# Other statistics, other chore slots and another split of the residual parts in a two-layer attention kernel

## The chip, the cores and the metric

The kernel runs on one core of a Trainium2 chip, in one launch. The metric is the time on the device in microseconds. A run of the kernel before takes 3205.84 us, the median of three runs (3205.17 to 3208.25). A core has five engines with a queue of instructions each: TensorE (PE; its weight loads are PEld), VectorE (DVE), ScalarE (ACT), GpSimd (POOL) and SyncE (SP). They wait for one another through semaphores, and the DMA transfers that SP and POOL issue run beside them.

## The reference

Two layers of the same kind are applied to x, 8 images of 512 channels by 32 x 32 pixels (1024 positions). All is float32. Cut to what matters, one layer is:

```python
xg = x.reshape(B, 8, -1)
xn = ((xg - xg.mean(-1)) * rsqrt(xg.var(-1) + 1e-5)).reshape(B, C, H, W) * gamma + beta
q, k, v = products of xn (512 channels) with wq, wk, wv (512 x 512), plus biases
attn = softmax(q.k / sqrt(64))          # 8 heads of 64 channels, 1024 x 1024 each
x = x + proj_w @ (attn @ v) + proj_b    # residual
```

The output is x after the second layer.

## The kernel before

**Jobs.** `jobs` lists 16 pairs of image and layer: images in twos, for each two both images in layer 0 and then both in layer 1. For every job n the main loop runs an attention and then the products of the next job: `v_phase` for V, and `deep_phases` for the output projection O of job n and for K and Q of job n + 1. The attention of job n is 64 iterations (8 groups of a pair of heads and half of the positions, 8 key blocks each): TensorE multiplies scores, ScalarE takes the exponential (L875, tile e), VectorE adds the exponentials up (L885, L887, tile acc), TensorE multiplies with the values (L901). At the end of a group VectorE reduces acc (L917) and adds the halves of the result (L924, into q). For each second group the row sums are brought together by small DMAs (r<-r, L944), VectorE inverts them (first L948), and they go out and back through rd and rb.

**Chores.** `put(i, fn)` hangs other work on iteration i of the attention, or on the next free one. This is how the next job's normalization is spread: `reads` (statistics of x and their gather), then `steps` (groups, factors, four applies that write xn), then the sums that the fast products need. Statistics come from VectorE (`stat`, BNStats on 512 positions, eight for each job), or for job 1 from ScalarE (`sums` and `squares`, four each, L244 and L252). `gather` sends them through DRAM: two DMAs mv to dm and one from dm to gm (L279), which waits for both. `groups` (L286 and after) works on gm and sends the result back as mr. In attentions 0 to 2 there are also factors for later use: `first_factors` loads blocks of a weight, VectorE makes four sums and differences of them (128 x 512, L154 to L160), and `store_factors` writes them to DRAM.

**Products.** O, K and Q are computed by a Strassen-like scheme at two levels: seven outer products, each a chain of seven inner ones. A set of 21 chains runs on TensorE, with two chains interleaved; chain c writes its result to tile p_c (128 x 1024) of the pool `epool`, tag e, which has six buffers and is shared with the exponentials. In a chain ScalarE writes three quarters of p (L646, L648) and copies one inner product to s, and VectorE writes the other quarters (L653, or L655 with a bias). When a chain's weights are used for the first time, `prepare` makes their inner differences on VectorE (four of 128 x 128, L154 to L160) and stores them as `deep`. Weights come from a ring of seven buffers.

**Residual.** The seven O tiles p_0 to p_6 (outer products 1, 2, 6, 5, 7, 3 and 4) are summed into quarters (oh, sh) of x. `end(c)` lists for each chain what it adds: `add` is a VectorE sum of two tiles (L668), `more(oh, sh, part)` adds part to a quarter of x, by VectorE (L684), or with `moved=True` by a DMA issued from GpSimd that accumulates in x (L682). VectorE's sums are put in the queue `outer`, and a thunk takes one of it after the inner products 7 and 3 of a chain, that is two for each chain. If `soon` (sums for O's right-hand sides) has something, that goes first; if `outer` is empty, `extra` is next: statistics of job n + 2 from chain 15 on, and after the attention of job 1 the loads and sums (L1081) of the second layer's output bias.

**Order.** Each engine runs its instructions in the order in which the program makes them. A tile of a pool can be written again only when its readers, DMAs too, are done; that is where waits on a buffer come from.

Of the kernel before, what the change touches and what calls it, by code (L numbers as in the profile page):

```python
# [28 lines left out]
NT = S // P  # L29
HALF = S // 2  # L30
HP = NH // 2
NVEC = 6 * NC
GAMMA, BETA, BQ, BK, BP, BV = (i * NC for i in range(6))
SUM_LIMIT = 1e10
# [38 lines left out]
def fast_path(  # L73
# [85 lines left out]
        else:  # L159
            nc.vector.tensor_sub(w[:, S4], w[:, A12], w[:, S2])  # L160

    def store_factors(w, layer, which):
        keep = wdram.tile([P, NW, 2, CH], F32, name=f"keep_{which}_{layer}")
        if (which, layer) == (O, 1):
            nc.sync.dma_start(keep, w)
        else:
            for s in (slice(S1, NW), slice(S3, S3 + 1)):
                nc.sync.dma_start(keep[:, s], w[:, s])
        factors[which, layer] = keep

    plan, held, raw = deque(), {}, set()
# [183 lines left out]
    def norm_steps(n):  # L355
        norm = Norm(n)

        def place():
            xn[0] = acts.tile([P, NC, S], F32, tag="xn", name=f"xn_{n}")

        def factors():
            norm.factors(slice(0, NC))
            if n > 1:
                place()

        if n == 1:
            reads = [place] + [lambda cc=cc: norm.sums(cc) for cc in range(NC)]
            reads.append(norm.less_mean)
            reads += [lambda cc=cc: norm.squares(cc) for cc in range(NC)]
            reads.append(lambda: (norm.by_count(), norm.gather()))  # L370
            return reads, [norm.groups, factors] + [lambda cc=cc: norm.apply(cc) for cc in range(NC)]
        reads = [lambda cc=cc, sh=sh: norm.stat(cc, sh) for cc in range(NC) for sh in range(2)]
        reads.append(norm.gather)
        steps = [norm.groups, factors] + [lambda cc=cc: norm.apply(cc) for cc in range(NC)]
        return reads, steps
# [198 lines left out]
    def deep_phases(n, extra, outs=None, early=()):  # L574
# [11 lines left out]
        def begin(c):  # L586
# [6 lines left out]
                (kt if which == K else qt)[0] = dst[which]  # L593
            if c + 2 < len(chains):
                ahead, oo = chains[c + 2]
                prepare((job(ahead), ahead, oo))
            if which == O and c in (3, 4):
                soon.extend(outs.steps(c + 2))
            e = epool.tile([P, 2, HALF], F32, tag="e", name=f"p_{n}_{c}")
# [59 lines left out]
        def end(c):  # L659
# [10 lines left out]
            if which == O:  # L670
                b, layer = jobs[m]
                xt = xs[b]

                def more(oh, sh, part, moved=False):


                    cols = slice(sh * HALF, (sh + 1) * HALF)
                    to_ = xt[:, 2 * oh : 2 * oh + 2, cols]

                    def go():  # L680
                        if moved:
                            nc.gpsimd.dma_start(to_, p(part), accum_op=ALU.add)  # L682
                        else:
                            nc.vector.tensor_add(to_, to_, p(part))  # L684
                        parts[oh, sh] -= 1
                        if layer == 1 and parts[oh, sh] == 0:
                            rows = slice(oh * CH, (oh + 1) * CH)
                            later(8.0 if moved else 2.0, lambda: nc.sync.dma_start(
                                out[b, rows, cols].rearrange("(c p) s -> p c s", p=P), to_
                            ))  # L690

                    if moved:
                        go()
                    else:
                        outer.append(go)

                if o == 1:
                    more(0, 0, 1, True)
                elif o == 2:
                    more(0, 0, 2, True)  # L700
                elif o == 6:
                    add(p(6), p(6), p(1))
                    more(0, 1, 6)
                elif o == 5:
                    more(0, 1, 5)
                    more(1, 1, 5, m in (0, 2))
                elif o == 7:
                    add(p(7), p(7), p(6))
                    more(1, 0, 7)
                    more(1, 1, 7)  # L710
                elif o == 3:
                    more(0, 1, 3, True)
                elif o == 4:
                    more(1, 0, 4, True)
                return
# [17 lines left out]
                add(quarter(1, 0), p(7), p(4))  # L733

        live, parts = {}, {(0, 0): 2, (0, 1): 3, (1, 1): 2, (1, 0): 2}
        soon, outer = deque(early), deque()

        def thunk(c, j):
            def go():
                if j == 0:  # L740
                    live[c] = begin(c)
                order = LAST_ORDER if c + 1 == len(chains) else ORDER
                live[c](order[j])
                if order[j] in (7, 3):
                    if soon:
                        soon.popleft()()
                    elif outer:
                        outer.popleft()()
                    elif extra and extra[0][0] <= c:
                        extra.popleft()[1]()  # L750
                if j == 6:
                    end(c)
                    if c + 1 == len(chains):
                        while outer:
                            outer.popleft()()
                advance(0.43)

            return go
# [334 lines left out]

        return load, [lambda oc=oc: add_up(oc) for oc in range(NC)]

    def first_factors(put, which_layers):

        box = []

# [3 lines left out]
                load_blocks(box[0][:, i], layer, which)  # L1103

        put(2, start)
        at = 9
        for i, (which, layer) in enumerate(which_layers):
            for part in range(4):
                at += 3
                put(at, lambda i=i, part=part: factor(box[0][:, i], part))  # L1110
            put(at + 1, lambda i=i, which=which, layer=layer: store_factors(
                box[0][:, i], layer, which
            ))

    deep_x, deep_t = [None], [None]
# [160 lines left out]
    for n in range(-1, len(jobs)):  # L1276
        last = n + 1 == len(jobs)
        outs = None
        if n >= 0:
# [10 lines left out]
                    put(44 + 3 * i, fn)  # L1290
            else:
                if n == 0:
                    first_factors(put, [(O, 0), (V, 1)])
                elif n == 1:
                    first_factors(put, [(K, 1), (Q, 1)])
                elif n == 2:
# [1 line left out]
                for i, (_, fn) in enumerate(extra):  # L1298
                    put(2 + i, fn)
                at = (10, 19, 22, 24, 26, 28, 36, 39, 42, 45)  # L1300
                if n == 0:
                    for i, fn in zip((3, 3, 4, 5, 6, 8, 10, 11, 12, 13, 15), reads):
                        put(i, fn)
                    at = (22, 30, 34, 35, 37, 38, 41, 44, 47, 50)
                for i, fn in zip(at, steps + sums(n + 1)):
                    put(i, fn)
                deep_first = deep_steps(n + 1)
                for at, fn in zip((52, 54, 57, 59), deep_first[4:]):
                    put(at, fn)
                put(61, lambda: (extend_plan(n + 1), [fetch() for _ in range(RING)]))  # L1310
            assert max(chores, default=0) < NT * len(att.groups)
# [16 lines left out]
            extra = deque()  # L1328
            if jobs[n][1] == 1 and jobs[n][0] + 2 < B:
                extra.append((11, lambda b=jobs[n][0] + 2: (x_tile(b), load_x(b))))  # L1330
            if n == 1:
                load, bias_steps = make_out_bias(1)
                extra.append((8, load))
                extra.extend((11, fn) for fn in bias_steps)
            if n + 2 < len(jobs):
                reads, steps = norm_steps(n + 2)
                extra.extend((15, fn) for fn in reads)
        both = deep_phases(n + 1, extra, outs, deep_first[:4] if outs else ())
        both[0]()
        rest[0]()  # L1340
# [259 lines left out]
```

## Time and profile before

Times in us, from the profiled execution. A stage reaches from the first exponentials of one attention to those of the next.

| What | Value |
|---|---|
| Profiled execution, its own time | 3206.06 |
| Its span | 3204.3 |
| Start, to the first attention | 81.57 |
| Attention of job 4 and the products after it (887.72 to 1085.57) | 197.85, TensorE busy all of it |
| Last stage (3064.17 on) | 140.83, TensorE busy 134.40 |
| Exponential L875, 128 x 1024 | 1024 of them, 1025 ns each |
| Sum of exponentials L887, 128 x 1024 | 768 of them, 1219 ns each |
| Sum of two product tiles L668, 128 x 1024 | 94 of them, 1214 ns each |
| Accumulating DMA x<-p, 512 KB | 62 of them, 6.9 from issue to landing in the median |

A row of the windows used below gives the length of a stretch and the busy time of each engine in it. A stage longer than its TensorE work holds waits of TensorE. Busy times of other engines count only where TensorE waits for them.

### The profile page before, as it was taken

The numbers are of one execution on the slowest core, as the hardware profiler recorded it, in microseconds if no ns is written. First come the engines' busy times: TensorE is split into PE (matmuls) and PEld (weight loads), VectorE is DVE, ScalarE is ACT, GpSimd is POOL, SyncE is SP. The second block draws the span as 40 slices with busy tenths as digits, with TensorE's granted clock in tenths as the row PEclk, the third lists the DMA queues.
The fourth block names the chain that finished last, engine by engine and source line by source line (L and its number), as shares of the span: only waits on it lengthen the run. The fifth ranks groups of instructions, "written<-read, shape, count | busy, mean of one in ns | idle before, by whom it ended". The sixth has DMA issues, their size and how long they took to land.

```text
span 3204.3 us, 57789 instructions
## 1 busy us (share of the span) xinstructions
PE 3185.3 (99%) x22917; PEld 1862.8 (58%) x22917; DVE 2772.8 (87%) x3989; ACT 1914.4 (60%) x3063; POOL 100.7 (3%) x95
## 2 busy tenths in 40 slices
PE   9999999999999999999999999999999999999999
PEld 7366384563836638366483754837547375573744
DVE  8897999979889798897988879888898888978878
ACT  4746646466565665656656565565656656566564
POOL 0000000000000000000000000000000000000000
PEclk9999999999999999999999999999999999999999
DMA  8234172350613305034170421504316051150611
GB/s 291 74 107 127 48 213 70 92 169 22 210 28 88 91 26 159 22 100 132 33 211 16 114 72 33 152 16 135 103 44 194 16 137 48 49 136 16 174 37 42
DMA packets 156998, 308.32 MB, mean 96 GB/s; under 512 B 34104, under 2 KB 60592, under 8 KB 156464
## 3 DMA queue, kind: packets, MB, share of 16 engines
q1 hardware_dynamic: 139856, 272.05, 26.8%
q0 software_dynamic: 16864, 32.51, 6.2%
q8 instruction: 181, 2.97, 0.4%
q14 instruction: 97, 0.79, 0.1%
HBM read 225.13 MB, written 45.68 MB: 85 GB/s over the span
## 4 chain that ended last, share of the span: by engine, by line
PE 95%; DVE 3%; DMA 1%; issue 0%; POOL 0%; ACT 0%; DVEq 0%; ACTq 0%; POOLq 0%
PE sc L870 28%; PE po L901 27%; PE zd L636 10%; PE vd L636 10%; PE z L494 6%; PE yd L636 5%; PE ud L636 4%; PE v L494 2%; PE y L494 2%; PE u L494 1%; PE z_last L814 0%; DMA x<-p 0%; DVE w L156 0%; DMA w<-deep 0%; DVE p L655 0%; DVE v L520 0%
## 5 line engine op out<-in xcount | busy, mean ns | idle before, releaser
L875 ACT ACTIVATE e<-sc 128x1024 f32<-128x1024 f32 x1024 | 1045.3, 1025 | 563.4 <-PE sc L870 457.4
L870 PE MATMUL sc<-q,k 64*64 64x512 f32 x8192 | 1058.0, 589 | 0.0
L901 PE MATMUL po<-e,v 64*64 64x512 f32 x8192 | 1057.1, 589 | 0.0
L887 DVE TENSOR_TENSOR acc<-acc,e 128x1024 f32<-128x1024 f32 x768 | 936.0, 1219 | 58.8 <-ACT e L875 12.1
L901 PEld LDWEIGHTS po<-e,v 64*64 64x64 f32 x8192 | 312.9, 133 | 566.0 <-issue 554.4
L870 PEld LDWEIGHTS sc<-q,k 64*64 64x64 f32 x8192 | 311.2, 133 | 562.7 <-issue 545.0
L885 DVE TENSOR_TENSOR acc<-e,e 128x1024 f32<-128x1024 f32 x128 | 156.3, 1221 | 112.3 <-ACT e L875 112.2
L636 PE MATMUL zd<-deep,w 128*128 128x256 f32 x860 | 241.1, 380 | 3.8 <-DVE p L653 1.7
L636 PE MATMUL vd<-deep,w 128*128 128x256 f32 x804 | 224.3, 380 | 2.1 <-DVE p L655 1.3
L636 PEld LDWEIGHTS zd<-deep,w 128*128 128x128 f32 x860 | 162.8, 190 | 28.2 <-DVE p L653 3.0
L636 PEld LDWEIGHTS vd<-deep,w 128*128 128x128 f32 x804 | 152.3, 190 | 24.6 <-DVE p L655 2.5
L917 DVE TRANSPOSE_TENSOR_REDUCE r<-acc 128x32 f32<-128x1024 f32 x128 | 158.5, 1238 | 0.6
L682 POOL DMA_DIRECT2D x<-p x62 | 74.6, 1211 | 1972.7 <-ACT p L646 1525.2
L636 PE MATMUL vd<-os,w 128*128 128x256 f32 x420 | 118.1, 380 | 1.6 <-DVE p L655 1.5
L668 DVE TENSOR_TENSOR p<-p,p 128x1024 f32<-128x1024 f32 x94 | 114.2, 1214 | 0.0
L494 PE MATMUL z<-w,t 128*128 128x256 f32 x480 | 110.9, 379 | 0.0
L494 PE MATMUL z<-w,xn 128*128 128x256 f32 x480 | 110.1, 382 | 0.0
L518 ACT COPY v<-z 128x512 f32<-128x512 f32 x32 | 18.8, 586 | 148.7 <-PE z L494 148.7
L494 PEld LDWEIGHTS z<-w,xn 128*128 128x128 f32 x480 | 90.0, 190 | 23.8 <-issue 12.2
L442 ACT COPY ud<-zd 128x256 f32<-128x256 f32 x156 | 55.7, 357 | 76.6 <-PE zd L636 75.1
L653 DVE TENSOR_TENSOR p<-vd,s 128x256 f32<-128x256 f32 x63 | 26.7, 424 | 85.6 <-PE vd L636 85.6
L657 ACT COPY s<-vd 128x256 f32<-128x256 f32 x156 | 58.1, 373 | 69.2 <-PE vd L636 69.2
(242 smaller groups left out, 4194.9 us busy)
## 6 DMA issues: line engine op xcount, KB each, us to landing
w<-deep SPq DMA_DIRECT2D x287, 448.0 KB, 3.8
x<-p POOLq DMA_DIRECT2D x62, 512.0 KB, 6.9
rb<-rd SPq DMA_DIRECT2D x96, 256.0 KB, 4.0
w<-keep SPq DMA_DIRECT2D x84, 256.0 KB, 2.7
deep<-w SPq DMA_DIRECT2D x42, 448.0 KB, 3.8
w<-wqkv_dram SPq DMA_DIRECT2D x57, 256.0 KB, 2.8
x<-x_dram SPq DMA_DIRECT2D x28, 512.0 KB, 6.4
out_dram<-x SPq DMA_DIRECT2D x28, 512.0 KB, 6.2
```

Source lines behind the costliest of these rows:

```text
L442: nc.scalar.copy(u, z)
L494: nc.tensor.matmul(ps[:, ti * CH : (ti + 1) * CH], right(src, tx[0], o)[:, cc, t0 : t0 + P], w[:, cc, :], start=(start and ti == 0 and cc ...
L636: nc.tensor.matmul(ps, lhs[:, FACTOR[i], :], moving[i], start=start, stop=True, skip_group_check=True,)
L657: return chain(product, lambda ps: nc.scalar.copy(s5, ps), put, z, y, u, w)
L668: outer.append(lambda: nc.vector.tensor_add(to_, a, b))
L682: nc.gpsimd.dma_start(to_, p(part), accum_op=ALU.add)
L870: nc.tensor.matmul(sc[h * HD : (h + 1) * HD, j, :], k[r, hp, k0 : k0 + HD], q[r, hp, sh * HALF : (sh + 1) * HALF], start=True, stop=True,)
L875: nc.scalar.activation(e, sc, AF.Exp, scale=SCALE)
L885: nc.vector.tensor_add(acc[g], self.es[i - 1], e)
L887: nc.vector.tensor_add(acc[g], acc[g], e)
L901: nc.tensor.matmul(po[g][j * HD : (j + 1) * HD, h, :], v[r, kc, d0 : d0 + HD], e[r, j, :], start=(kc == 0), stop=(kc == NT - 1),)
L917: nc.vector.tensor_reduce(self.r[:, 0, m, :], self.acc.pop(g).rearrange("p j (b e) -> p (j b) e", e=RP), AX.X, ALU.add, apply_transpose=True,)
```

## The change

It has these parts:

- Job 3's statistics too come from ScalarE (`ALONE`), and the chore positions that go with that are used for both jobs, 1 and 3. Several of them are a little earlier, and in attention 0 the sums for the next products come at 39 to 45 and 47 to 53.
- In attention 0 the factors are made at every second chore from 8 on, no longer every third from 12; `store_factors` issues these stores, and those of the later attentions, on GpSimd's queue.
- After the attention of job 0, x's quarter (0, 0) gets its first part by VectorE, (0, 1) gets part 5 by DMA and (1, 1) gets part 5 by VectorE. Parts by DMA are no longer issued at once where another part of the same quarter is still waiting in `outer`; they keep their place behind it (`waiting`, `free`).
- Preparations of K's and Q's weights go to a queue `made`, which is served after inner product 7; `soon` and `outer` are served after 3, or when `made` is empty.
- The second layer's output bias is loaded and summed after the attention of job 0, no longer of job 1.

```diff
@@ -29,6 +29,7 @@
 NT = S // P
 HALF = S // 2
 HP = NH // 2
+ALONE = (1, 3)
 NVEC = 6 * NC
 GAMMA, BETA, BQ, BK, BP, BV = (i * NC for i in range(6))
 SUM_LIMIT = 1e10
@@ -159,13 +160,13 @@
         else:
             nc.vector.tensor_sub(w[:, S4], w[:, A12], w[:, S2])
 
-    def store_factors(w, layer, which):
+    def store_factors(w, layer, which, queue=nc.sync):
         keep = wdram.tile([P, NW, 2, CH], F32, name=f"keep_{which}_{layer}")
         if (which, layer) == (O, 1):
-            nc.sync.dma_start(keep, w)
+            queue.dma_start(keep, w)
         else:
             for s in (slice(S1, NW), slice(S3, S3 + 1)):
-                nc.sync.dma_start(keep[:, s], w[:, s])
+                queue.dma_start(keep[:, s], w[:, s])
         factors[which, layer] = keep
 
     plan, held, raw = deque(), {}, set()
@@ -360,10 +361,10 @@
 
         def factors():
             norm.factors(slice(0, NC))
-            if n > 1:
+            if n not in ALONE:
                 place()
 
-        if n == 1:
+        if n in ALONE:
             reads = [place] + [lambda cc=cc: norm.sums(cc) for cc in range(NC)]
             reads.append(norm.less_mean)
             reads += [lambda cc=cc: norm.squares(cc) for cc in range(NC)]
@@ -593,7 +594,11 @@
                 (kt if which == K else qt)[0] = dst[which]
             if c + 2 < len(chains):
                 ahead, oo = chains[c + 2]
-                prepare((job(ahead), ahead, oo))
+                key = (job(ahead), ahead, oo)
+                if key in raw and n > 0 and ahead != O:
+                    made.append(lambda: prepare(key))
+                else:
+                    prepare(key)
             if which == O and c in (3, 4):
                 soon.extend(outs.steps(c + 2))
             e = epool.tile([P, 2, HALF], F32, tag="e", name=f"p_{n}_{c}")
@@ -683,27 +688,32 @@
                         else:
                             nc.vector.tensor_add(to_, to_, p(part))
                         parts[oh, sh] -= 1
+                        waiting[oh, sh] -= 1
                         if layer == 1 and parts[oh, sh] == 0:
                             rows = slice(oh * CH, (oh + 1) * CH)
                             later(8.0 if moved else 2.0, lambda: nc.sync.dma_start(
                                 out[b, rows, cols].rearrange("(c p) s -> p c s", p=P), to_
                             ))
 
-                    if moved:
+                    waiting[oh, sh] += 1
+                    if not moved:
+                        outer.append(go)
+                    elif waiting[oh, sh] == 1:
                         go()
                     else:
                         outer.append(go)
+                        free.append(go)
 
                 if o == 1:
-                    more(0, 0, 1, True)
+                    more(0, 0, 1, m > 0)
                 elif o == 2:
                     more(0, 0, 2, True)
                 elif o == 6:
                     add(p(6), p(6), p(1))
                     more(0, 1, 6)
                 elif o == 5:
-                    more(0, 1, 5)
-                    more(1, 1, 5, m in (0, 2))
+                    more(0, 1, 5, m == 0)
+                    more(1, 1, 5, m == 2)
                 elif o == 7:
                     add(p(7), p(7), p(6))
                     more(1, 0, 7)
@@ -733,7 +743,8 @@
                 add(quarter(1, 0), p(7), p(4))
 
         live, parts = {}, {(0, 0): 2, (0, 1): 3, (1, 1): 2, (1, 0): 2}
-        soon, outer = deque(early), deque()
+        waiting, free = dict.fromkeys(parts, 0), []
+        soon, outer, made = deque(early), deque(), deque()
 
         def thunk(c, j):
             def go():
@@ -742,10 +753,16 @@
                 order = LAST_ORDER if c + 1 == len(chains) else ORDER
                 live[c](order[j])
                 if order[j] in (7, 3):
-                    if soon:
+                    if made and order[j] == 7:
+                        made.popleft()()
+                    elif soon:
                         soon.popleft()()
                     elif outer:
                         outer.popleft()()
+                        while outer and outer[0] in free:
+                            outer.popleft()()
+                    elif made:
+                        made.popleft()()
                     elif extra and extra[0][0] <= c:
                         extra.popleft()[1]()
                 if j == 6:
@@ -1093,7 +1110,7 @@
 
         return load, [lambda oc=oc: add_up(oc) for oc in range(NC)]
 
-    def first_factors(put, which_layers):
+    def first_factors(put, which_layers, at=9, apart=3):
 
         box = []
 
@@ -1103,13 +1120,12 @@
                 load_blocks(box[0][:, i], layer, which)
 
         put(2, start)
-        at = 9
         for i, (which, layer) in enumerate(which_layers):
             for part in range(4):
-                at += 3
+                at += apart
                 put(at, lambda i=i, part=part: factor(box[0][:, i], part))
             put(at + 1, lambda i=i, which=which, layer=layer: store_factors(
-                box[0][:, i], layer, which
+                box[0][:, i], layer, which, nc.gpsimd
             ))
 
     deep_x, deep_t = [None], [None]
@@ -1290,7 +1306,7 @@
                     put(44 + 3 * i, fn)
             else:
                 if n == 0:
-                    first_factors(put, [(O, 0), (V, 1)])
+                    first_factors(put, [(O, 0), (V, 1)], 6, 2)
                 elif n == 1:
                     first_factors(put, [(K, 1), (Q, 1)])
                 elif n == 2:
@@ -1298,14 +1314,14 @@
                 for i, (_, fn) in enumerate(extra):
                     put(2 + i, fn)
                 at = (10, 19, 22, 24, 26, 28, 36, 39, 42, 45)
-                if n == 0:
+                if n + 1 in ALONE:
                     for i, fn in zip((3, 3, 4, 5, 6, 8, 10, 11, 12, 13, 15), reads):
                         put(i, fn)
-                    at = (22, 30, 34, 35, 37, 38, 41, 44, 47, 50)
+                    at = (22, 30, 34, 35, 36, 37, 39, 41, 43, 45)
                 for i, fn in zip(at, steps + sums(n + 1)):
                     put(i, fn)
                 deep_first = deep_steps(n + 1)
-                for at, fn in zip((52, 54, 57, 59), deep_first[4:]):
+                for at, fn in zip((47, 49, 51, 53) if n == 0 else (52, 54, 57, 59), deep_first[4:]):
                     put(at, fn)
                 put(61, lambda: (extend_plan(n + 1), [fetch() for _ in range(RING)]))
             assert max(chores, default=0) < NT * len(att.groups)
@@ -1328,13 +1344,14 @@
             extra = deque()
             if jobs[n][1] == 1 and jobs[n][0] + 2 < B:
                 extra.append((11, lambda b=jobs[n][0] + 2: (x_tile(b), load_x(b))))
-            if n == 1:
+            if n == 0:
                 load, bias_steps = make_out_bias(1)
-                extra.append((8, load))
-                extra.extend((11, fn) for fn in bias_steps)
+                extra.append((9, load))
+                extra.extend((12, fn) for fn in bias_steps)
             if n + 2 < len(jobs):
                 reads, steps = norm_steps(n + 2)
-                extra.extend((15, fn) for fn in reads)
+                if n + 2 not in ALONE:
+                    extra.extend((15, fn) for fn in reads)
         both = deep_phases(n + 1, extra, outs, deep_first[:4] if outs else ())
         both[0]()
         rest[0]()
```

## The prediction

> **What bounds the kernel now.** I read the page first, its span, its engines and its chain of waits:
>
> ```profile
> span 3204.3 us, 57789 instructions
> PE 3185.3 (99%) x22917; PEld 1862.8 (58%) x22917; DVE 2772.8 (87%) x3989; ACT 1914.4 (60%) x3063; POOL 100.7 (3%) x95
> ...
> PE 95%; DVE 3%; DMA 1%; issue 0%; POOL 0%; ACT 0%; DVEq 0%; ACTq 0%; POOLq 0%
> ...
> x<-p POOLq DMA_DIRECT2D x62, 512.0 KB, 6.9
> ```
>
> TensorE sets the end. So I cut the span at the first exponential of each attention and took busy time by stage (window, length, then PE, PEld, DVE, ACT, POOL, clock, DMA share, GB/s):
>
> ```profile
> 81.57:287.13 205.56, 199.89 (x1435) 115.30 (x1437) 179.02 (x274) 127.34 (x208) 8.25 (x6) 1.00 0.37 107
> 287.13:489.78 202.65, 199.95 (x1435) 115.30 (x1437) 188.52 (x311) 119.63 (x192) 6.22 (x5) 1.00 0.40 122
> 489.78:689.87 200.09, 198.76 (x1435) 115.67 (x1437) 178.16 (x270) 119.72 (x192) 7.43 (x6) 1.00 0.40 124
> 689.87:887.72 197.85, 197.85 (x1434) 115.85 (x1437) 170.54 (x238) 119.73 (x192) 6.22 (x5) 1.00 0.34 99
> ```
>
> Each row is the same TensorE work, one attention and the products after it. From the fourth on it takes 197.85 us with TensorE never idle. The first three exceed this by 7.71, 4.80 and 2.24: 14.75 us together, 0.46% of the run. The change moves work in these three alone (TensorE's order is untouched), so no gain can pass 14.75 us. The waits of TensorE in the first two windows (total, times, longest):
>
> ```profile
> PE zd L636 <- DVE p L653: 1.7, 2, 1.1
> PE v L494 <- DVE q L924: 1.7, 1, 1.7
> PE zd L636 <- ACT yd L438: 1.6, 1, 1.6
> PE vd L636 <- DVE p L655: 0.6, 1, 0.6
> ```
>
> ```profile
> PE vd L636 <- DVE p L655: 1.1, 3, 0.6
> PE zd L636 <- DVE p L655: 0.7, 1, 0.7
> PE zd L636 <- DVE p L653: 0.6, 1, 0.6
> ```
>
> These total less than the excess, since a stalled matmul also looks longer; start-to-start distances of TensorE against the usual 0.216 us give the rest. Then VectorE in attention 0, VectorE in the second set of products, and GpSimd's transfers in both sets:
>
> ```profile
> DVE lt L948 <- DMA r<-r: 2.5, 1, 2.5
> ```
>
> ```profile
> 440.66 1.21 DVE L684 TENSOR_TENSOR x<-x,p 128x1024 f32<-128x1024 f32 x1
> 441.80 0.47 DVE L655 SCALAR_TENSOR_TENSOR p<-ud,out_step,s 128x256 f32<-128x256 f32 x1
> 442.19 1.21 DVE L684 TENSOR_TENSOR x<-x,p 128x1024 f32<-128x1024 f32 x1
> 443.32 0.28 DVE L154 TENSOR_TENSOR w<-w 128x128 f32<-128x128 f32 x1
> ```
>
> ```profile
> 235.10 2.44 POOL L682 DMA_DIRECT2D x<-p  x2 [9.55 <-DVE os L539]
> 240.77 1.20 POOL L682 DMA_DIRECT2D x<-p  x1 [3.23 <-ACT p L648]
> 245.59 1.20 POOL L682 DMA_DIRECT2D x<-p  x1 [3.62 <-ACT p L648]
> ```
>
> ```profile
> 442.81 1.20 POOL L682 DMA_DIRECT2D x<-p  x1 [9.05 <-ACT yd L438]
> 447.93 1.20 POOL L682 DMA_DIRECT2D x<-p  x1 [3.92 <-DVE w L156]
> ```
>
> VectorE lies end to end at 440 us: two big adds (1.13 us each from start to start) and a weight preparation (four differences, 0.93 us with their waits) for every chain of seven products, which takes TensorE 3.02 us.
>
> [...] the second row agrees (199.95 busy where 197.85 is needed), so I count window lengths. [...] The trace has 6.9 in the median and 7.7 to 11.0 in the first set, and I use these. [...]
>
> **The change, part by part.**
>
> *Attention 0.* The stores of factors leave SP's queue, the r gather of L944 is no longer behind the wait for dm's landing, and the 2.5 us wait at L948 goes. Squares, gather() and groups() move: by_count and gather go from chore 16 to 21, groups from 23 to 24. Groups thus comes 3 iterations (1.72 us each, 5.1 us) after gather. In the trace the first dm was issued at 110.43, gm at 116.76 (it waits for dm's landing) and gm takes some 2.3 us to land: 8.6 us, and a set of rd and rb DMAs now stands between the dm issues on SP. I place gm's landing at 130.4 to 131.9, VectorE at L286 at 124.7: a new wait of 5.7 to 7.2 us, queued in front of every acc add. Factors done sooner fill idle time that VectorE had before. The last acc add (195.61 in the trace) then comes at 196.9 to 198.4, as VectorE is never idle after the wait. The V products wait for it: TensorE loses 3.1 to 4.6 us where it lost 1.93; I take 3.8. Late acc adds hold e's buffers for some 0.5 (0.1 to 1.0). Moving the stores itself I cost at nothing: GpSimd is idle there (3%); if not hidden, 1.2 us of GpSimd each, which nobody awaits.
>
> *First products (0 to 1).* Gone: p_6's write waiting for the transfer of p_1 (1.84 on TensorE with its restart) and quarter (1,1)'s add waiting for that of p_3 (1.34). Staying: 2.4 of waits on VectorE's backlog (0.27, 0.33, 0.90, 0.90). New, since (0,0) gets p_0 by VectorE and p_1 by DMA after it: p_7 takes p_1's buffer, whose transfer now starts after the add of chain 4, 0.6 (0 to 1.9); p_9 takes p_3's, 0.15 (0 to 0.3); p_11 takes p_5's, whose transfer must follow p_3's into the same quarter, 1.4 (0.4 to 4.3); p_12 takes p_6's, 0.3 (0 to 0.6). The ends are the 7.7 and 11.0 us of landing, less ScalarE's slack of 0.66 (its wait of 2.43 cost TensorE 1.74 plus restart). Four L1081 sums and 1.25 MB of rows move here; they replace normalization statistics that go to attention 1, so VectorE's load stays: nothing, or 0.68 each if they meet the backlog; I leave that in the range.
> Sum: 3.8 + 0.5 + 2.4 + 0.6 + 0.15 + 1.4 + 0.3 = 9.15 against 7.71.
>
> *Attention 1.* Two more BNStats (0.60 each) and a gather 3.4 us later: VectorE waits 1.7 to 3.4 us at L286. Its idle time of 1.33 at 316.7 and 1.0 at 344.2 comes later in this attention and takes most of it up: 0.25 (0 to 0.5).
>
> *Second products (1 to 2).* Preparations in K and Q alternate with adds, one add per chain in place of two: 0.93 + 1.13 + two put adds (0.33 to 0.40) = 2.8 us, under 3.02. So the 4.80 goes, and the sums and L1081s leave. What is late next: the adds. x's add of p_3 ends near 445.2, so p_5's transfer starts at 445.7 in place of 442.81; with 6.1 to 9.7 us it lands at 451.8 to 455.4, p_9 needs the buffer at 450.5, less 0.66: 2.5 (0.8 to 4.4). The add of p_4 moves to chain 9, p_6's transfer lands at 464 to 467 where p_12 needs it at 462: 2.6 (1.3 to 4.3). ScalarE meets VectorE's adds at six more tiles, within its slack: 0.3 (0 to 1).
> Sum: 0.25 + 2.5 + 2.6 + 0.3 = 5.65 against 4.80.
>
> *Third stage.* Job 3's statistics go to ScalarE (four sums, four squares at 1.1 to 1.2 us with ScalarE 60% busy): 0.1. The O preparations' waits (two of 0.8) stay: 2.35 against 2.24. Later stages: nothing.
>
> **Sum.** 9.15 + 5.65 + 2.35 = 17.15, which is 2.4 us above 14.75. The profiled execution's own time is 3206.06 (span 3204.3 and 1.8 around it), the median 3205.84: 3208.3 on the median, 3208 said.
>
> **Rivals.** *Faster:* transfers land in 5.4 to 6.1 us, as the first two of the second set did, and gm is there when VectorE comes. Then the losses are 1.9 + 2.4 + 0.5 in the first stage, 0.8 in the second, 2.3 in the third: 7.9, so 3199. Against it: two DMA waits one after the other lie between gather and L286 in every job of the trace (8 to 10 us). *Slower:* GpSimd's queue of x's parts becomes the bound. Each transfer now starts after a VectorE add, and holds one of six buffers. With landings of 10 us throughout, the five terms above take their upper ends: 1.9 + 0.3 + 4.3 + 0.6 + 4.4 + 4.3 = 15.8 for 7.55, so 3216; it decides from landings of about 9 us, and the moved 1.25 MB speaks for it. *It only moves:* VectorE's relief and the late adds cancel in each stage, 3206; this is the forecast's neighbour, and what it means is that the waits changed names.
>
> **Chances.** 0.2% (6.4 us) is about what a measurement of this kernel can tell from no change. Forecast 0.38, moves only 0.12, faster rival 0.17, slower rival 0.33. The forecast alone spans 3200 to 3214; with the rivals 3198 to 3217. Faster 0.17, same 0.5, slower 0.33.
>
> **What would show it.** Right: the 2.5 us at L948 gone and VectorE waiting over 5 us for gm at L286 in attention 0; "v L494 <- DVE q" longer; no wait of p L648 in the first set for p_1 at chain 6; the VectorE waits of the second set replaced by waits on yd L438 at chains 9 and 12. Wrong: a first window under 204 us (gm in time), a second under 199 (transfers hidden), or a third or fourth window that changes by over 1 us.

## The result and the profile after

The changed kernel takes 3217.07 us (median of 7 runs, 3216.08 to 3217.89) against 3204.95 for the kernel before in the same runs: a ratio of 1.0036, with a 95% interval of 1.0027 to 1.0046. It is slower by some 12 us. Its profiled execution took 3217.07. Lines of the changed kernel are its own: the exponential is L892, the product matmul L641, the residual's transfer L687, `groups` begins at L287.

The head of the page:

```profile
span 3215.3 us, 57810 instructions
...
PE 3188.8 (99%) x22917; PEld 1862.4 (58%) x22917; DVE 2770.2 (86%) x3980; ACT 1920.8 (60%) x3079; POOL 103.1 (3%) x103
```

TensorE has 3.5 us more busy time with the same matmuls, and 11.0 us more span. The stages, cut as before (columns: window, length, busy time of PE, PEld, DVE, ACT and POOL, clock, DMA share, GB/s):

```profile
82.20:296.57 214.37, 203.28 (x1435) 115.06 (x1436) 181.39 (x282) 126.88 (x208) 8.73 (x9) 0.98 0.36 106
296.57:497.01 200.44, 198.98 (x1435) 115.30 (x1436) 184.04 (x297) 118.59 (x192) 8.43 (x9) 1.00 0.40 117
497.01:701.12 204.11, 200.45 (x1435) 115.09 (x1436) 177.05 (x267) 127.56 (x208) 7.93 (x7) 1.00 0.40 122
701.12:898.98 197.86, 197.86 (x1435) 116.07 (x1437) 170.61 (x238) 119.72 (x192) 6.14 (x5) 1.00 0.34 99
```

The first stage is 8.8 us longer than before, the second 2.2 shorter, the third 4.0 longer: 10.6 of the span's 11.0. All later ones are the same within 0.1 us. The clock column of the first row, 0.98, was 1.00 before. TensorE's waits in the first stage:

```profile
PE sc L887 <- ACT e L892: 4.9, 1, 4.9
PE vd L641 <- ACT yd L439: 1.9, 2, 1.3
PE zd L641 <- ACT yd L439: 1.5, 1, 1.5
PE v L495 <- DVE q L941: 1.1, 1, 1.1
...
```

One wait of 4.9 us stands at the scores, inside attention 0, where TensorE had never stopped. Who caused it is read from three timelines of the same stretch (start, duration, what it is, idle time before and its releaser). In the kernel before, both dm DMAs go out together, and VectorE comes to `groups` 16 us later and doesn't wait. SP's and VectorE's lines of it:

```profile
110.43 1.36 SPq L275 DMA_DIRECT2D dm<-mv  x2
116.76 0.38 SPq L279 DMA_DIRECT2D gm<-dm  x1
126.71 0.21 DVE L286 BATCH_NORM_STATS2 gs<-gm 8x6 f32<-8x64 f32 x1
```

In the changed kernel, SP's:

```profile
122.50 0.68 SPq L276 DMA_DIRECT2D dm<-mv  x1
123.28 2.49 SPq L980 DMA_DIRECT2D rb<-rd  x2
125.82 1.39 SPq L276 DMA_DIRECT2D dm<-mv  x1
134.15 0.36 SPq L280 DMA_DIRECT2D gm<-dm  x1
```

VectorE's:

```profile
124.20 1.22 DVE L904 TENSOR_TENSOR acc<-acc,e 128x1024 f32<-128x1024 f32 x1
137.25 0.22 DVE L287 BATCH_NORM_STATS2 gs<-gm 8x6 f32<-8x64 f32 x1 [11.83 <-DMA gm<-dm]
```

ScalarE's:

```profile
131.36 1.02 ACT L892 ACTIVATE e<-sc 128x1024 f32<-128x1024 f32 x1 [0.69 <-PE sc L887]
139.36 1.94 ACT L892 ACTIVATE e<-sc 128x1024 f32<-128x1024 f32 x2 [6.98 <-DVE acc L902]
```

Read backwards. ScalarE could not write the next exponential for 6.98 us, as all six buffers held exponentials that VectorE had not added. VectorE stood 11.83 us at `groups`, which needs gm. SP could issue gm only at 134.15, when the second dm had landed, 8.3 us after its issue; and that issue had come 3.3 us after the first, behind rb's two. TensorE's next scores waited for ScalarE in turn. When it went on, its clock was half for four more microseconds. Two windows of the changed kernel, with the columns of the stages (the clock stands third from the end):

```profile
140.40:144.60 4.20, 4.16 (x20) 1.28 (x24) 4.09 (x5) 1.93 (x2) 0.00 (x0) 0.52 0.03 5
144.60:149.00 4.40, 4.40 (x48) 1.53 (x44) 4.03 (x7) 2.53 (x3) 0.00 (x0) 1.00 0.00 0
```

20 score and value matmuls in 4.2 us, then 48 in 4.4. Start-to-start distances give 5.0 us for the stall and 2.0 for the slow matmuls.

### The profile page after: what moved, and what is told of

It is laid out like the page before. It is cut to its first block, busy times and chain, and to the rows that moved or that the text cites. A ratio compares the mean times of both kernels' runs of the same rounds, so it can differ in the third digit from the quotient of the medians.

```text
span 3215.3 us, 57810 instructions
## 1 busy us (share of the span) xinstructions
PE 3188.8 (99%) x22917; PEld 1862.4 (58%) x22917; DVE 2770.2 (86%) x3980; ACT 1920.8 (60%) x3079; POOL 103.1 (3%) x103
## 4 chain that ended last, share of the span: by engine, by line
PE 88%; DVE 2%; DMA 1%; issue 0%; ACT 0%; SPq 0%; DVEq 0%; ACTq 0%; POOLq 0%
PE sc L887 25%; PE po L918 25%; PE vd L641 9%; PE zd L641 9%; PE z L495 6%; PE yd L641 5%; PE ud L641 4%; PE u L495 1%; PE y L495 1%; PE v L495 1%; DVE acc L904 1%; DMA x<-p 1%; PE z_last L831 0%; DMA w<-deep 0%; PE u_last L831 0%
## 5 line engine op out<-in xcount | busy, mean ns | idle before, releaser
L892 ACT ACTIVATE e<-sc 128x1024 f32<-128x1024 f32 x1024 | 1044.5, 1024 | 563.3 <-PE sc L887 451.4
L641 PE MATMUL zd<-deep,w 128*128 128x256 f32 x860 | 240.7, 380 | 3.0 <-ACT yd L439 2.7
L641 PE MATMUL vd<-deep,w 128*128 128x256 f32 x804 | 224.6, 380 | 3.4 <-ACT yd L439 2.1
L641 PEld LDWEIGHTS zd<-deep,w 128*128 128x128 f32 x860 | 163.0, 190 | 26.5 <-ACT yd L439 3.9
L641 PEld LDWEIGHTS vd<-deep,w 128*128 128x128 f32 x804 | 151.9, 190 | 26.9 <-ACT yd L439 4.5
L687 POOL DMA_DIRECT2D x<-p x61 | 72.3, 1193 | 1929.8 <-ACT p L651 1591.8
L641 PE MATMUL vd<-os,w 128*128 128x256 f32 x420 | 118.3, 380 | 1.4 <-DVE p L660 1.3
```

The source lines that it names most:

```text
L641: nc.tensor.matmul(ps, lhs[:, FACTOR[i], :], moving[i], start=start, stop=True, skip_group_check=True,)
L892: nc.scalar.activation(e, sc, AF.Exp, scale=SCALE)
```

## The experiments

Twelve kernels ran. "Stage" is the time between the first exponentials of consecutive attentions in the profile; before they are 205.56, 202.65 and 200.09, in the changed kernel 214.37, 200.44 and 204.11. In the diffs, "-" is the changed kernel unless said otherwise.

### Factors at their old chores

```diff
-                    first_factors(put, [(O, 0), (V, 1)], 6, 2)
+                    first_factors(put, [(O, 0), (V, 1)])
```

> The changed kernel, with the factors of attention 0 at every third chore from 12 on, as before. Theory 1 (VectorE's wait of 11.8 us for gm in attention 0 stops ScalarE and TensorE, and the wait is there because the crowded chores push gather to chore 21): gather returns to 16, the wait for gm is under 1 us, the stall of 4.9 us at the scores and the slower clock after it go, the first stage falls from 214.4 to about 207.5, the run to 3209 to 3211. Theory 2 (GpSimd's transfers of x's parts are the cost): nothing of that depends on the factors, 3216 to 3218. Two groups of four factors end later here, and may push the last sum of exponentials by 0.5 us.

Measured: 3209.25 us (3206.58 to 3212.08). The first dm was issued at 110.36, VectorE came to `groups` at 126.39 without any wait, and the stage took 207.67. The stall and the slow clock are gone (1.00 over the stage), 6.7 of the stage's 8.8 us with them. Theory 1 holds, theory 2 doesn't.

### Applies and sums at their old chores

```diff
-                    at = (22, 30, 34, 35, 36, 37, 39, 41, 43, 45)
+                    at = (22, 30, 34, 35, 37, 38, 41, 44, 47, 50)
...
-                for at, fn in zip((47, 49, 51, 53) if n == 0 else (52, 54, 57, 59), deep_first[4:]):
+                for at, fn in zip((52, 54, 57, 59), deep_first[4:]):
```

> The changed kernel, with the chores of both ScalarE-normalized jobs at the positions of before: applies at 34, 35, 37, 38, the sums at 41 to 50 and 52 to 59. Theory 3 (four applies of 1.13 us in consecutive iterations, each with an exponential of 1.02 us, exceed the iteration of 1.72 us): the scores stop waiting for ScalarE at the applies in attentions 0 and 2, 1.1 and 1.4 us less, the run 3214 to 3215. Theory 1 with VectorE's lag as the only limit: the sums come later, the last sum of exponentials does not move, 3216.5 to 3217.5. If the sums come too late, the wait of V's products grows by up to 1 us and eats the gain.

Measured: 3220.44 us, a miss in sign. In attention 0 the small waits at the applies did go, but the wait for gm was still there (12.67) and VectorE, with its sums later, ended later: V's products waited 2.09 us in place of 1.14, and the clock was 0.51 for 3.5 us after it. In the six other traces that have this wait for gm (11.83 to 12.79) and keep the early sums, V's products waited 1.13 to 1.15, so the earlier sums of the change were worth about 1 us. First stage 217.05. In attention 2 the waits at the applies stayed (1.26 us). The third stage, 208.20, has a wait for a weight of 2.5 us near its end, which is not explained.

### Job 3's statistics by VectorE

```diff
-ALONE = (1, 3)
+ALONE = (1,)
```

> The changed kernel, with ScalarE's statistics for job 1 alone and job 3's by VectorE as before. If the 4.0 us of the third stage come from the four applies and from VectorE's waits for r and rb in attention 2, the stage returns from 204.1 to 200.1 and the run to 3213. If they come from the sums of x that the second set of products now does later, the stage stays at 204 and the run at 3217. The second set gets eight BNStats of 0.6 us back in its last chains: up to 1 us there.

Measured: 3219.31 us (3216.54 to 3220.22; the profiled execution 3216.54). Third stage 204.06, unchanged, but its make-up is another: nothing at the applies, 3.35 us at V's products in place of 1.49. VectorE waits 4.2 us for gm and 2.7 for rb there. The change of engine neither helped nor hurt; the cause had to be something that both have.

### The shares of x as before

```diff
-                    more(0, 0, 1, m > 0)
+                    more(0, 0, 1, True)
...
-                    more(0, 1, 5, m == 0)
-                    more(1, 1, 5, m == 2)
+                    more(0, 1, 5)
+                    more(1, 1, 5, m in (0, 2))
```

> The changed kernel, with the shares of x's quarters after job 0 as before (first part of (0,0) by DMA, part 5 of (0,1) by VectorE and of (1,1) by DMA), and the new queueing of parts kept. Theory 2 (GpSimd's transfers are the main cost): the first stage falls by 4 us or more, the run under 3213. Theory 1: the three waits on buffers, 3.9 us together, go, and the two waits of before, 3.1 us, come back: the stage within 1.5 us of 214.4, the run 3215.5 to 3218.

Measured: 3216.57 us, first stage 213.61. The waits on p's buffers go (1.66, 0.77 and 1.44 us of TensorE), and the two of before come back (1.32 and 1.66). The new shares cost 0.8 us, no more: GpSimd's transfers are not the main cost.

### Without the alternation

```diff
-                if key in raw and n > 0 and ahead != O:
+                if False:
```

> The changed kernel, with K's and Q's weights prepared at the beginning of a chain as before, so that they no longer alternate with x's sums. If the alternation is what freed VectorE in the second set of products, its waits of 0.3 to 0.9 us for p come back and the second stage rises from 200.4 to 202 or more (before: 202.65), the run to 3218.5 to 3219.5. Rival: the output bias's sums, which left that set, freed it; then the stage stays under 201 and the run at 3217.

Measured: 3217.64 us. The second stage is 200.79, the rival's number. VectorE's waits did come back, 0.25 to 0.70 us four times, but the two waits on buffers of the changed kernel (below) went. The alternation exchanges one for the other at nearly equal cost (200.44 with it).

### The stores on SP's queue

```diff
-                box[0][:, i], layer, which, nc.gpsimd
+                box[0][:, i], layer, which, nc.sync
```

> The changed kernel, with the factors' stores on SP's queue again. If GpSimd's store of 124.6 to 131.5 us slows the statistics' small transfers (the second dm took 8.3 us to land), that store now stands behind gm in SP's queue, gm comes at least 2 us sooner, the wait at L287 falls from 11.8 to 9 or less, and the first stage to 211 or less. If the time lies in SP's order (rd, dm, two rb, dm, gm) and in dm itself, the wait stays between 11 and 13 and the stage at 214 to 215.5. The third stage: within 0.5 of 204.1 either way.

Measured: 3213.79 us (3212.81 to 3214.89). In the first stage (214.72) the wait for gm stays, 11.97, so GpSimd's stores had nothing to do with it. The third stage was expected to stay and did not:

```profile
497.40:698.00 200.60, 199.24 (x1435) 115.48 (x1434) 176.88 (x266) 127.41 (x208) 7.43 (x6) 1.00 0.40 124
```

(The window of that stage, columns as above.) It is 3.5 us less than in the changed kernel. What differs is where the store of the last factors (L166, all seven blocks in one transfer) stands against rb. GpSimd's timeline of the changed kernel:

```profile
540.31 0.58 POOL L166 DMA_DIRECT2D keep<-raw  x1 [73.49 <-DVE raw L161]
```

VectorE's timeline of the changed kernel, where it needs rb:

```profile
548.95 1.23 DVE L995 TENSOR_TENSOR q<-q,rb 128x1024 f32<-128x1024 f32 x1 [2.75 <-DMA rb<-rd]
```

SP's timeline of the kernel with the stores on its queue:

```profile
540.52 1.31 SPq L980 DMA_DIRECT2D rb<-rd  x2
541.88 0.58 SPq L166 DMA_DIRECT2D keep<-raw  x1
```

On GpSimd's queue the store starts beside rb (issued at 540.01 and 540.70), and the second rb lands 8.2 us after its issue; VectorE waits 2.75 us for it. On SP's queue the store comes behind both, and that wait is gone. The end of the sums lags the last exponential by 4.5 us in place of 6.4, and V's products, which waited 1.5 us, don't wait. The three later kernels with these stores on SP's queue have third stages of 200.28 to 201.50; with the stores on GpSimd's queue none is under 203.19.

### The alternation alone

Against the kernel before; the thunk takes from `made` after inner product 7, as in the change.

```diff
-                prepare((job(ahead), ahead, oo))
+                key = (job(ahead), ahead, oo)
+                if key in raw and n > 0 and ahead != O:
+                    made.append(lambda: prepare(key))
+                else:
+                    prepare(key)
```

> The kernel before with one part of the change alone: K's and Q's preparations alternate with the sums (made). First stage 205.6 as before. Second stage 200.4 to 201.5 instead of 202.65. Third stage: job 3's BNStats come last in the second set and are pushed into attention 2; if that costs what the run with ALONE for job 1 showed, the wait of V's products for q returns with 2.5 to 3.5 us and the stage is 202.5 to 203.5, the run 3204.5 to 3206. If it is not the pushed statistics that cost the third stage, it stays at 200.1 and the run is 3202.5 to 3203.5.

Measured: 3220.68 us, far from what was expected. First stage 204.96; second 204.91, longer than before; third 212.42. TensorE's waits in the last two:

```profile
PE sc L878 <- ACT e L883: 10.9, 1, 10.9
PE zd L640 <- DVE p L657: 5.4, 2, 4.8
```

In the second stage a sum into x waits 5.7 us for a transfer into the same quarter, with the puts queued behind it. In the third, the pushed statistics end so late that gather (530.59) comes just before `groups` and factors: VectorE waits 4.65 us for gm and ScalarE 11.86 for the factors (L306), at the head of its queue, the exponentials behind. The alternation alone is a loss. That it needs what the change moved out of that set, or the new place of the transfers behind waiting parts of the same quarter, is likely and was not tested.

### The output bias after job 1

```diff
-            if n == 0:
+            if n == 1:
                 load, bias_steps = make_out_bias(1)
-                extra.append((9, load))
-                extra.extend((12, fn) for fn in bias_steps)
+                extra.append((8, load))
+                extra.extend((11, fn) for fn in bias_steps)
```

> The changed kernel, with the output bias's loads (1 MB of rows and bv) and sums after job 1 again. If these loads slow the transfers of x's parts in the first set (p_3's took 11.5 us to land, p_6's 10.1), these fall to 6 to 8 us, the three waits on buffers (3.9 us together) shrink by at least 2 us and the first stage to 212.5 or less. If the waits come from the order alone (p_1's transfer after the sum of p_0, p_5's after p_3's), they stay above 3 us and the stage above 213.3. The second stage gets four sums of 0.7 us back: 200.4 to 201.2.

Measured: 3220.19 us, stages 212.26, 200.73 and 209.03. GpSimd's timeline in the first set of the changed kernel:

```profile
248.76 1.20 POOL L687 DMA_DIRECT2D x<-p  x1 [1.82 <-DVE p L660]
260.88 2.40 POOL L687 DMA_DIRECT2D x<-p  x2 [10.91 <-DVE p L658]
```

The same of this kernel:

```profile
249.47 1.20 POOL L687 DMA_DIRECT2D x<-p  x1 [1.82 <-DVE p L660]
258.42 2.40 POOL L687 DMA_DIRECT2D x<-p  x2 [7.75 <-ACT ud L443]
```

The transfer of p_3 landed after 8.4 us in place of 11.5, and p_5's, into the same quarter, started that much sooner. Of the waits on buffers one of 1.12 us is left. p_6's transfer did not change (10.1 and 10.2). In the changed kernel the rows are loaded at 248.68 and 251.70, beside the transfer of p_3. This run moves loads and sums together; as the time is that of the transfer itself, from issue to landing, the loads are the likely reason. The third stage was not foreseen: the bias's sums, pushed into attention 2, push its gather to 538.17, and VectorE waits 9.45 us for gm at `groups`, and TensorE 4.2 us at the scores. It is the fault of attention 0 again, in another attention.

### Statistics first, factors around them

The puts of `reads` for ScalarE's jobs stand before `first_factors`, so that they get their chores and the factors the free ones.

```diff
+                if n + 1 in ALONE:
+                    for i, fn in zip((3, 3, 4, 5, 6, 8, 10, 11, 12, 13, 15), reads):
+                        put(i, fn)
                 if n == 0:
                     first_factors(put, [(O, 0), (V, 1)], 6, 2)
...
-                    for i, fn in zip((3, 3, 4, 5, 6, 8, 10, 11, 12, 13, 15), reads):
-                        put(i, fn)
```

> The changed kernel, with the chores of ScalarE's statistics placed before those of the factors, so that sums, squares and gather of attention 0 keep the chores of before (gather at 15 to 16) and the factors of every second chore give way to them; in attention 2 likewise. Theory 1 (the distance from gather to groups decides): the wait for gm in attention 0 falls from 11.8 us to under 2, the stall of 4.9 us and the slow clock go, the first stage is 206.5 to 208.5 and the run 3208 to 3211, although the factors are still done sooner. Rival (the factors' early load on VectorE is itself the trouble): the stage stays over 211.

Measured: 3208.32 us (3206.73 to 3210.05), the first stage 204.72, less than expected and less than before. The wait for gm is 0. And V's products wait 0.2 us for q, where the run with the old chores of the factors had 2.0. TensorE's waits in its first stage:

```profile
PE vd L641 <- ACT yd L439: 1.8, 2, 1.6
PE zd L641 <- ACT yd L439: 1.1, 1, 1.1
PE vd L641 <- DVE p L660: 0.6, 1, 0.6
PE zd L641 <- DVE p L658: 0.6, 1, 0.6
PE v L495 <- DVE q L941: 0.2, 1, 0.2
```

Factors sooner is a gain if gather keeps its place: the stage is 2.9 us under the run with the old chores, 1.8 of it at V's products. The distance to `groups` decides, not VectorE's early load.

### Three tries for a kernel better than both

Factors' chores, stores' queue and shares of before, the rest of the change kept:

```diff
-                    first_factors(put, [(O, 0), (V, 1)], 6, 2)
+                    first_factors(put, [(O, 0), (V, 1)])
...
-                box[0][:, i], layer, which, nc.gpsimd
+                box[0][:, i], layer, which, nc.sync
...
-                    more(0, 0, 1, m > 0)
+                    more(0, 0, 1, True)
...
-                    more(0, 1, 5, m == 0)
-                    more(1, 1, 5, m == 2)
+                    more(0, 1, 5)
+                    more(1, 1, 5, m in (0, 2))
```

> The changed kernel with three parts undone: the factors at every third chore, their stores on SP's queue, the shares of x's quarters after job 0 as before. Kept are ScalarE's statistics for job 3, the alternation of preparations and sums, the queueing of parts and the bias after job 0. First stage 206.0 (207.7 of the run with the factors' slots less the 0.8 that the shares gave, and a little more or less), second 200.6 to 200.9, third 200.6: sum 1.0 under before's 608.3, the run 3203.5 to 3205.5. If the stores on GpSimd's queue were not what cost the third stage, it stays at 203 to 204 and the run is 3207.

Measured: 3205.20 us against 3205.43, ratio 0.9999 (0.9991 to 1.0007). Stages 206.55, 200.94, 200.72.

Factors' chores and stores' queue of before, the bias later in the first set:

```diff
-                extra.append((9, load))
-                extra.extend((12, fn) for fn in bias_steps)
+                extra.append((13, load))
+                extra.extend((15, fn) for fn in bias_steps)
...
+                if n == 1:
+                    at = (14, 21, 23, 25, 27, 29, 36, 39, 42, 45)
```

> The changed kernel with the factors' slots and the stores' queue of before, the output bias's loads at chain 13 and its sums at chain 15 of the first set (9 and 12 in the change), and in attention 1 groups at chore 14 and the applies from 23 on, since its statistics come later. The new shares are kept. If the bias's loads are what makes the transfers of x's parts late, the waits on buffers in the first set fall from 3.9 us to about 1.1 and the first stage to 203.5 to 204.5; second 200.4 to 201, third 200.6: the run 3201 to 3203, under before. If the statistics that are pushed into attention 1 meet a wait for gm there, the second stage grows to 203 or more.

Measured: 3206.50 us, ratio 1.0002 (0.9994 to 1.0011). Stages 206.76, 201.75, 200.28. The edit did not do what it says: rows were loaded at 240.9 and 244.0, chain 8 as in the changed kernel, for on SP's queue the loads did not follow the new due chain; only the sums moved. It says nothing about the loads.

Statistics first, as above, and the stores on SP's queue, all else of the change kept:

```diff
-                box[0][:, i], layer, which, nc.gpsimd
+                box[0][:, i], layer, which, nc.sync
```

> The changed kernel with the statistics' chores placed before the factors' and the factors' stores on SP's queue; all other parts of the change kept. First stage 204.5 to 205.5 (204.7 with the statistics first), second 200.8 to 201.4, third 200.3 to 200.9 if GpSimd's store in attention 2 is what cost it 3.5 us (204.2 if not): together 1.5 to 2.5 under before's 608.3, the run 3202.5 to 3204.5. If SP's queue with the stores delays gather again, the first stage is 206 or more and the run no better than before.

Measured: 3204.57 us (3202.96 to 3209.01) against 3205.38, ratio 0.9998 (0.9990 to 1.0007). The windows of its first three stages:

```profile
81.10:286.60 205.50, 200.33 (x1435) 115.06 (x1434) 181.61 (x281) 126.76 (x208) 6.45 (x5) 1.00 0.38 111
286.60:487.10 200.50, 198.91 (x1431) 115.06 (x1430) 184.04 (x296) 118.50 (x192) 6.22 (x5) 1.00 0.40 116
487.10:688.60 201.50, 199.56 (x1431) 115.28 (x1430) 176.87 (x266) 127.26 (x208) 7.43 (x6) 1.00 0.40 124
```

These are 0.8 us under before together, too little for the runs to show. Mending two faults of the change gives back its 12 us. No version measurably better than the kernel before was found.

## Why the prediction was right or wrong

The forecast was 3208, its range reached 3217 and the chance of slower was 0.33. The time, 3217.07, lies at the range's very end. The forecast had the three stages 9.15, 5.65 and 2.35 us above their TensorE work; they are 16.52, 2.59 and 6.26 above it. So the sum missed three quarters of the loss. Step by step:

- **What bounds the kernel.** Right. The three stages hold 10.6 of the 11.0 us, and later ones are the same within 0.1 us.
- **Attention 0, the place.** Right: a new wait at L287 for gm, because gather is put off to chore 21. The old wait at L948 for r went, as forecast. The queue of the stores had no part in it: with the stores on GpSimd's queue and gather at its old place the wait was 2.27 again (the run with the old chores of the factors).
- **Attention 0, the size.** This is the step that failed. gm was priced at 8.6 us from the first dm, from a trace in which both dm DMAs are issued together; the rd and rb DMAs between them were named and hardly priced. It took 14.7 (122.50 to 137.23), so the wait was 11.83 and not 5.7 to 7.2. Where both dm DMAs went out together and VectorE waited for gm (attentions 1 and 2 of several runs), it got gm 7.5 to 9.4 us after the first dm (8.0 in attention 1 of the changed kernel, from 310.16), so 8.6 was right for that case. That the second dm landed late because rb's transfers stood ahead of it is likely, but was not tested alone.
- **Attention 0, what is late next.** Also wrong. The delay was carried to the end of the attention and charged to V's products, at 3.8 us, with 0.5 for the buffers. But a wait of 11.83 us lasts for seven iterations, and six buffers don't cover these: TensorE stood 5.0 us in the middle, and lost 2.0 more at a slow clock that nothing before had shown. V's products then waited less than before, 1.14 us. At the four applies, which the change puts into consecutive iterations (34 to 37), another 1.1 us was lost. But these slots alone cost nothing: two variants with gather at its old place (the old chores of the factors, the statistics first) keep them, and their TensorE doesn't wait anywhere in attention 0. The loss comes only where VectorE is late already. In attention 2 the same loss, 1.3 us, goes away with the stores on SP's queue.
- **First products.** The buffers' waits were placed right. Terms: p_7 0 (0.6 said), p_9 1.66 (0.15), p_11 0.77 (1.4), p_12 1.44 (0.3); 3.9 us for 2.45. The bias, left in the range at nothing, made the difference: with it back after job 1 one wait of 1.12 is left.
- **Second products.** 2.59 us over 197.85, against 5.65. The two new waits on yd L439 came at the places named, with 1.39 and 0.41 for 2.5 and 2.6. That the alternation frees VectorE was seen, but the stage doesn't hang on it: without it the stage is 200.79, and with it alone 204.91. Nor does it hang on the bias's leaving alone, which the prediction had put in one half-sentence: with the bias back after job 1 it is 200.73, though part of its work then slips into attention 2. With job 3's statistics back it is 200.78. No single part brings 202.65 back; which of them together shortened the stage stays open. In attention 1 the wait at L287 was 1.64 us and cost TensorE nothing (0.25 said).
- **Third stage.** 6.26 against 2.35. The failing step is "Moving the stores itself I cost at nothing". It was argued from GpSimd's idle time, and the cost is on the DMA side. Before, SP issued the store at 531.09, behind both rb DMAs (from 529.68), and VectorE did not wait for rb; in the changed kernel GpSimd issued it at 540.31, between rb's two, and the second rb landed after 8.2 us. Moving the store to another queue took away the order in which these transfers had been issued. The run with SP's queue puts 3.5 us on this.
- **The slower rival** had the time, 3216, by another mechanism: transfers of x's parts, with 15.8 us of waits. They made 5.7 (3.9 and 1.8), and undoing the shares moved the run by half a microsecond. That its number fits is luck. (Its "five terms" are six; their sum, 15.8, is right.)

## What to carry to other kernels

When work is put into the slots between long chains, look at what it displaces: the distance from a gather through DRAM to its reader is part of the schedule, and here it shrank from 16 us to 3 by work that was nowhere near it in the code. Compare a wait on an in-order engine first with the time that its consumers' buffers cover (six exponentials of 1.72 us here): well below, the wait was pushed to the end here; near it or above, it stopped the bounding engine. In attention 2, 4.2 us for gm became 3.35 us at V's products (job 3 by VectorE), while 9.45 us stopped the scores for 4.2 us (the bias after job 1), and 11.83 us in attention 0 for 4.9. And price a DMA that changes its queue by what it now runs beside (the second rb took 8.2 us with the store issued before it), not by the issuing engine's idle time.

## What the runs showed of the hardware

I had not expected the slow clock. It comes on top of a stall, and not after every stall. From 20 us to 3200 the granted clock was 1.00 throughout in the kernel before; in the changed kernel it was 1.00 too, but for one stretch at 0.50, from 137.62 to 144.44. That lies around the stall from 135.59 to 140.44 (busy PE is the first number after the length, the clock stands third from the end):

```profile
134.20:137.61 3.41, 1.39 (x16) 0.23 (x8) 0.32 (x3) 0.00 (x0) 0.00 (x0) 1.00 0.01 1
137.62:141.03 3.41, 0.59 (x4) 0.31 (x8) 3.34 (x8) 1.67 (x2) 1.48 (x1) 0.50 0.00 0
141.03:144.44 3.41, 3.41 (x20) 0.97 (x16) 3.31 (x3) 1.30 (x2) 0.00 (x0) 0.50 0.04 6
144.45:147.86 3.41, 3.41 (x36) 1.15 (x32) 3.10 (x4) 2.37 (x3) 0.00 (x0) 1.00 0.00 0
```

In the kernel with the alternation alone, around a stall from 446.96 to 451.77, the clock was still 1.00 up to 452.37, and 0.50 in the 3.41 us after it:

```profile
445.54:448.95 3.41, 1.42 (x7) 0.92 (x5) 0.00 (x0) 0.88 (x3) 0.84 (x1) 1.00 1.08 223
448.96:452.37 3.41, 0.60 (x3) 0.55 (x4) 2.18 (x6) 0.00 (x0) 0.00 (x0) 1.00 1.11 236
452.37:455.78 3.41, 3.41 (x10) 2.67 (x9) 2.44 (x7) 1.21 (x3) 0.00 (x0) 0.50 0.67 218
```

The length of a stall alone doesn't tell whether the clock falls. With the old applies V's products waited 2.09 us, and the clock was 0.51 in the 3.5 us after it (207.8 to 211.3). With the old chores of the factors they waited 2.0 us, and it stayed at 1.00 (197 to 202). With job 3 by VectorE they waited 3.35 us in attention 2, and it stayed at 1.00 as well (612 to 623). What decides it was not shown.

Estimated as half of TensorE's busy time in the slow stretch, the extra loss was 2.0 us in the changed kernel (4.00 us busy, 137.62 to 144.44), 1.7 at V's products with the old applies (3.48 us, 207.8 to 211.3) and 1.4 after the stall of attention 0 with the bias after job 1 (2.83 us at 0.52, 141.1 to 144).
